# Layers 1 and 2 of a four-layer graph network: values and scores by seven block products, and six graphs in flight

## The chip, the cores and the metric

The kernel runs on one NeuronCore of a Trainium2 chip. The metric is the device time of one execution in microseconds (us). Before the change it is 2376.73 us, the median of 3 runs (2376.35 to 2377.58).

## What is computed

The input is 32 graphs of 512 nodes with 256 features (`x`, float32) and a 512x512 adjacency of zeros and ones with about 3% ones (`adj`, int32). Four layers follow each other, each of the form `x = x + layer(relu(layernorm(x)), adj)`; the layers differ. Layer 0 is softmax attention with two convolutions, layer 3 has a full bilinear score. Layers 1 and 2 are the ones that the change touches:

```
# layer 1                                   # layer 2
Wh = h @ W.T                                Hh = h @ W
src, dst = Wh @ a1, Wh @ a2                 s, d = Hh @ a_src, Hh @ a_dst
e = leaky(src[:,None] + dst[None,:])        e = exp(-leaky(s[:,None] + d[None,:]))
e = where(adj > 0, e, -9e15)                e = where(adj != 0, e, 0)
x = x + softmax(e) @ Wh                     x = x + elu((e @ Hh) / rowsum(e))
```

For each node a layer needs a value row (256 numbers) and two scores. Both are one product: the weight matrix is widened by two columns, W times a1 and W times a2, so that `h @ [W | Wa]` gives 258 columns.

## The kernel before, in words

A node tile is 128 nodes on 128 partitions, so a graph has NT = 4 tiles; the features are HC = 2 halves of 128. Everything is float32 on the TensorE. One Python function, `graph(b, ...)` (L467), lists the work of graph b as operations with an engine, a cost, what they follow, and the buffers that they use. A planner (`Plan`, L53) then lays all 32 graphs out: `order` (L131) keeps a clock per engine, gives each operation a due time worked back from its graph's number, and takes on each engine the most urgent operation whose inputs and buffers are there. The costs of L32 to L50 and the `SLACK` factors of L67 are what it plans with. The result is a fixed order of instructions for each engine; on the chip each engine goes through its own list in that order, and waits on semaphores.

The buffers are counted. `slot` (`FLIGHT` = 5, L243) says how many graphs may be between their first step and their store; `ahead` is one more and is for inputs loaded early. 35 `page`s of 4 KB for each partition hold nearly everything: x, normalized rows, transposed features, masks, exponentials. `v` are 4 value buffers, `bank` the 8 PSUM banks.

**One layer of a graph.** `normed` (L527) makes statistics on VectorE, a power on GpSimd, the normalized rows on ScalarE, and transposes them through a split into 16-bit planes (VectorE L551), a DMA transpose (SP queue, L554) and a join on ScalarE (L566) into `hT`. For layers 1 and 2, `scored_values` (L659) then makes four products, one for each node tile and all independent of each other: two accumulating matmuls of 258 columns (L669) into one PSUM bank, from which ScalarE copies 256 columns of values to `v` (L676) and VectorE the two score columns to a score buffer (L673). `leaky_exp_t` (L683) makes a row of scores over all nodes: in most graphs VectorE transposes 32x32 blocks (L697), and a DMA writes the row to DRAM (L701) and another spreads it to all partitions (L706); in the first two and last two graphs TensorE transposes instead (L693). ScalarE adds the other score and applies the leaky slope (L710) and the exponential (L713). VectorE masks: layer 1 takes the minimum with `mask1` (L934), a tile that VectorE makes once for each graph out of the transposed codes `codeT` (L931); layer 2 compares the codes directly (L961). `attend` (L726) multiplies: for each of 4 node tiles four times one matmul of 257 columns (L736; 256 values and a column of ones that yields the row sum).

**Products by blocks.** The other products (layer 0's and all of layer 3's) use `seven` (L592): a product of 2x2 blocks with seven block products in place of eight, in two PSUM banks p and q. Its order is fixed: product 1 into p, out; product 6 onto p, out; product 7 onto p, out; product 4 onto p, out, each waiting until the one before has been copied out of p by ScalarE; products 2, 5 and 3 go into q, and VectorE adds q onto the blocks. `block_sums` (L624) makes the four sums of input blocks that this needs, on VectorE (L639), three of them one after another. `seven_of` (L388) makes the seven weight blocks once at the start. `by_nodes` (L779) is the block product with nodes as rows: two matmuls of 128 or 129 columns (L783).

A float32 `nc.tensor.matmul` call leaves two MATMUL records and two LDWEIGHTS records in the trace, so a count in the profile is twice the number of calls.

Of the kernel before, what the change touches and what calls it, by code (L numbers as in the profile page):

```python
# [11 lines left out]
F32 = mybir.dt.float32  # L12
# [7 lines left out]
P = 128  # L20
# [4 lines left out]
HUGE = 2.0**100  # L25
# [27 lines left out]
class Plan:  # L53
# [13 lines left out]
    SLACK = {"V": (1.05, 0.0), "A": (1.05, 0.0), "G": (1.5, 0.0), "D": (1.0, 800.0)}  # L67
# [138 lines left out]
def kernel(  # L206
# [36 lines left out]
    FLIGHT = 5  # L243
    PAGES, VALUES = 35, 4
# [107 lines left out]

    def transposed(w_sb, dst, after, *keys):
        done = []
        for c in range(HC):
            key = f"bank{next(banks)}"

            def turn(c, key):
                for r in range(HC):
                    nc.tensor.transpose(W[key][:, r * P : (r + 1) * P], w_sb()[:, r, c * P : (c + 1) * P], ident)  # L360

            def out_of(c, key):
                nc.vector.tensor_copy(dst()[:, c, :], W[key][:, : HC * P])
# [45 lines left out]
    l1_aug, l2_aug = (tile_of(n, H + 2) for n in ("l1_aug", "l2_aug"))  # L409
# [5 lines left out]
    for n, dst, w, key in (("w0", w0_s, w0, "raw9"), ("att", att_s, att_w, "raw10")):  # L415
# [9 lines left out]
    l3_wide = raw("raw8", H + 2)  # L425
    a = [load(l1_sb, rows_of(l1_w), "raw0")]
    ready["l1"] = transposed(l1_sb, lambda: l1_aug[:, :, :H], a, "raw0")
    a += [load_column(l1_ac, l1_a.rearrange("n o -> (n o)"))]
    ready["l1"] += product(lambda d: l1_aug[:, d, H : H + 2], l1_sb,
                           lambda c: l1_ac.rearrange("p (o c) -> p c o", o=2)[:, c, :], 2, a, "raw0")  # L430
    a = [load(l2_aug[:, :, :H], rows_of(l2_w))]
    a = ready["l2"] = a + transposed(lambda: l2_aug[:, :, :H], l2_wt, a, "raw1")
    a = a + [load_column(l2_ac, l2_a.rearrange("o n -> (o n)"))]
    ready["l2"] = a + product(lambda d: l2_aug[:, d, H : H + 2], l2_wt,
                              lambda c: l2_ac.rearrange("p (o c) -> p c o", o=2)[:, c, :], 2, a, "raw1")
# [23 lines left out]

    score_bufs = []  # L460
    for i in range(FLIGHT):
        s = const.tile([P, P + NT], F32, tag=f"scores{i}", name=f"scores{i}")
        nc.gpsimd.memset(s, 0.0)
        score_bufs.append(s)


    def graph(b, adj_before, x_before):  # L467
# [42 lines left out]
        def classes(g):  # L510
            nc.vector.tensor_scalar(T["code"][:, two(g), :], T["adj"][:, two(g), :], -1.0, 2.0, ALU.max, ALU.min)
# [9 lines left out]
        def mask0():  # L521
            nc.vector.tensor_scalar(T["mask0"], T["codeT"], 1.0, TINY, ALU.is_equal, ALU.max)
# [132 lines left out]
        def scores_of():  # L655

            return score_bufs[T.places["slot"]["number"]]
# [528 lines left out]
```

## Time and profile before

| | |
|---|---|
| median of 3 runs | 2376.73 us |
| the profiled execution, its own time | 2375.45 us |
| its span, first to last instruction | 2373.7 us |
| mean granted TensorE clock | 0.999 |
| busy: TensorE, VectorE, ScalarE, GpSimd | 2347.7, 2056.8, 1720.1, 251.6 us |
| share of the span | 99%, 87%, 72%, 11% |
| chain that ended last, by engine | PE 94%, DVE 3%, ACT 2% |
| moved by DMA | 178.72 MB, mean 75 GB/s |

Times in the profile are of one execution. The profile has, first, busy time for each engine, and the span in 40 slices with the busy tenths of each engine in each. PE is TensorE's matmuls, PEld its weight loads, DVE VectorE, ACT ScalarE, POOL GpSimd, and SP the engine that issues most DMAs. Then come groups of instructions: line, engine, operation, what is written and read, shape and count, the busy time, the mean length of one in ns, and the idle time ahead of them with what ended it. "Busy" counts time in which at least one instruction of an engine is under way, so two that overlap are not counted twice, and a mean length can be more than the step from one start to the next. The timeline merges equal neighbours into one line with a count. The table of stretches gives each engine's busy time and, in brackets, its number of instructions between two times. A wait names the engine that ended it.

### The profile page before, as it was taken

What the parts mean: (1) busy time and instruction counts of PE and PEld (TensorE: products, weight loads), DVE (VectorE), ACT (ScalarE), POOL (GpSimd) and SP (SyncE); (2) the same over time, 40 slices, a digit from 0 to 9 for tenths busy, and PEclk for the clock granted to TensorE, in tenths of its full rate; (3) what the DMA queues carried; (4) which work ended last, traced back from release to release, by engine and by line L of the source; (5) the groups of instructions that cost most, each with busy time, mean ns of one, the idle gap of its engine ahead of it and who ended that gap; (6) DMA issues with size and microseconds to landing.
All of it is one profiled execution on the core that took longest, in us unless ns stands there. A gap on an engine that the chain in (4) does not pass through costs nothing.

```text
span 2373.7 us, 36569 instructions
## 1 busy us (share of the span) xinstructions
PE 2347.7 (99%) x11590; PEld 1985.6 (84%) x11590; DVE 2056.8 (87%) x6330; ACT 1720.1 (72%) x3386; POOL 251.6 (11%) x319
## 2 busy tenths in 40 slices
PE   7999999999999999999999999999999999999998
PEld 5887888888888888888888888888888888888887
DVE  6787899888898888988888988889888889888799
ACT  4566777777777777777777777777777777766785
POOL 3000010111001010101110111001011100100110
PEclk9999999999999999999999999999999999999999
DMA  7421332333333233332323334233233333321221
GB/s 188 94 54 30 87 86 65 85 79 69 85 70 89 69 67 87 78 84 70 85 61 85 74 72 87 65 85 78 66 88 77 71 83 74 89 54 41 49 47 43
DMA packets 432017, 178.72 MB, mean 75 GB/s; under 512 B 386288, under 2 KB 403824, under 8 KB 431824
## 3 DMA queue, kind: packets, MB, share of 16 engines
q1 hardware_dynamic: 426464, 158.03, 29.8%
q0 software_dynamic: 5216, 18.23, 2.3%
q8 instruction: 92, 1.51, 0.3%
q14 instruction: 101, 0.83, 0.1%
q10 hardware_dynamic: 144, 0.13, 0.0%
HBM read 67.64 MB, written 16.89 MB: 36 GB/s over the span
## 4 chain that ended last, share of the span: by engine, by line
PE 94%; DVE 3%; ACT 2%; DMA 0%; issue 0%; SPq 0%; POOL 0%; DVEq 0%; ACTq 0%
PE bank_a L736 35%; PE bank_z L893 9%; PE bank_v L669 9%; PE bank_o L911 5%; PE bank_s3p L1025 5%; PE bank_q0p L848 4%; PE bank_f3p L757 4%; PE bank_v0p L783 4%; PE bank_f0p L757 4%; PE bank_w3p L783 4%; PE bank_q0q L848 3%; PE bank_s3q L1025 3%; PE bank_v3p L783 2%; PE bank_v3q L783 2%; ACT e L710 1%; ACT e L713 0%
## 5 line engine op out<-in xcount | busy, mean ns | idle before, releaser
L736 PE MATMUL bank_a<-v,e 128*128 128x257 f32 (+1 forms) x4096 | 979.8, 381 | 6.0 <-DVE e L823 3.0
L736 PEld LDWEIGHTS bank_a<-v,e 128*128 128x128 f32 x4096 | 758.3, 190 | 155.3 <-issue 55.3
L566 ACT COPY hT<-planesT 128x512 uint16<-128x512 uint16 x508 | 380.8, 766 | 52.0 <-DMA planesT<-planes 51.6
L539 POOL TENSOR_TENSOR rstd<-ve,mhalf 128x2 f32<-128x2 f32 x256 | 215.9, 871 | 1875.1 <-DVE ve L536 1584.4
L546 ACT ACTIVATE xn<-x,off,rstd 128x256 f32<-128x256 f32 x512 | 276.0, 596 | 39.2 <-DVE off L542 39.0
L669 PE MATMUL bank_v<-l_aug,hT 128*128 128x258 f32 x1024 | 252.8, 381 | 2.1 <-ACT e L710 1.1
L893 PE MATMUL bank_z<-e,y 128*128 128x512 f32 x512 | 240.6, 592 | 0.0
L551 DVE COPY planes<-xn 128x512 uint16<-128x512 uint16 x508 | 205.7, 418 | 23.0 <-DMA planesT<-planes 17.2
L669 PEld LDWEIGHTS bank_v<-l_aug,hT 128*128 128x128 f32 x1024 | 191.7, 190 | 30.5 <-ACT e L710 1.5
L532 DVE BATCH_NORM_STATS2 st<-x 128x6 f32<-128x256 f32 x512 | 209.0, 408 | 4.1 <-DMA x<-in_x_dram 4.0
L710 ACT ACTIVATE e<-row,scores 128x512 f32<-128x512 f32 x224 | 150.7, 713 | 16.3 <-DMA row<-row 16.0
L893 PEld LDWEIGHTS bank_z<-e,y 128*128 128x128 f32 x512 | 96.9, 190 | 68.0 <-issue 57.9
L713 ACT ACTIVATE e<-e 128x512 f32<-128x512 f32 x256 | 150.3, 624 | 0.0
L676 ACT COPY v<-bank_v 128x256 f32<-128x256 f32 x256 | 90.2, 376 | 71.5 <-PE bank_v L669 67.7
L911 PE MATMUL bank_o<-w_sb,zT 128*128 128x256 f32 x512 | 116.2, 379 | 0.0
L1032 DVE SCALAR_TENSOR_TENSOR e<-bank_s3p,v,mask 128x256 f32<-128x256 f32 x256 | 111.2, 476 | 2.7 <-PE bank_s3p L1025 1.9
L533 DVE BATCH_NORM_AGGREGATE mv<-st 128x2 f32<-128x6 f32 x512 | 93.1, 182 | 17.5
L911 PEld LDWEIGHTS bank_o<-w_sb,zT 128*128 128x128 f32 x512 | 97.0, 190 | 13.4
L1077 ACT ACTIVATE e<-e 128x512 f32<-128x512 f32 x128 | 78.1, 629 | 22.7 <-DVE e L1074 22.0
L915 DVE SCALAR_TENSOR_TENSOR z<-bank_o,rs,b_sb 128x256 f32<-128x256 f32 x128 | 56.0, 479 | 40.7 <-PE bank_o L911 40.1
L974 ACT ACTIVATE y<-bank_a,rs 128x256 f32<-128x256 f32 x128 | 54.7, 476 | 49.4 <-DVE rs L970 25.9
L1071 ACT ACTIVATE e<-e,zero 128x512 f32<-128x512 f32 x128 | 84.9, 711 | 6.6 <-DVE crest L1049 6.6
(189 smaller groups left out, 4414.9 us busy)
## 6 DMA issues: line engine op xcount, KB each, us to landing
adj<-in_adj_dram SPq DMA_DIRECT2D x128, 256.0 KB
x<-in_x_dram SPq DMA_DIRECT2D x31, 512.0 KB
out_dram<-y POOLq DMA_DIRECT2D x31, 512.0 KB, 3.5
row<-row SPq DMA_DIRECT2D x56, 256.0 KB
planesT<-planes SPq DMA_TRANSPOSE x508
codeT<-code SPq DMA_TRANSPOSE x128
crest<-crest SPq DMA_TRANSPOSE x64
row<-sT SPq DMA_DIRECT2D x56, 2.0 KB
```

Of the source, the lines that this page charges most:

```text
L532: nc.vector.bn_stats(T[f"st{l}"][:, t, :], T["x"][:, t, :])
L539: nc.gpsimd.tensor_tensor(T[f"rstd{l}"][:, two(g)], T[f"ve{l}"][:, two(g)], mhalf[:, two(g)], ALU.pow)
L546: nc.scalar.activation(T[f"xn{l}"][:, t, :], T["x"][:, t, :], AF.Relu, bias=T[f"off{l}"][:, t : t + 1], scale=T[f"rstd{l}"][:, t : t + 1])
L551: nc.vector.tensor_copy(T[f"planes{l}_{t}"], bits)
L566: nc.scalar.copy(bits[:, :, :, t * P : (t + 1) * P], T[f"planesT{l}_{t}"].rearrange("p (b c) n -> p b c n", b=2))
L669: nc.tensor.matmul(T[key][:, :cols], T[f"hT{l}"][:, c, t * P : (t + 1) * P], w_aug[:, c, :], start=(c == 0), stop=(c == HC - 1))
L736: nc.tensor.matmul(T[key][:, : LEAD + H + 1 - lead], e(l, c)[:, t * P : (t + 1) * P], T[f"v{l}"][:, c, lead:], start=(c == 0), stop=(c == ...
L757: nc.tensor.matmul(p[:, : N // 2], w[:, x - 1, :], right(x), start=fresh, stop=True, skip_group_check=True)
L783: nc.tensor.matmul(p[:, j * k : (j + 1) * k], right(x)[:, j * P : (j + 1) * P], w[:, x - 1, :], start=fresh and j == 0, stop=True, skip_gr ...
L893: nc.tensor.matmul(T[f"bank_z{k}"], T["y0"][:, c, k * P : (k + 1) * P], e(0, c), start=(c == 0), stop=(c == NT - 1))
L911: nc.tensor.matmul(T[key][:, j * H : (j + 1) * H], T["zT"][:, k, t * P : (t + 1) * P], w1_sb[:, k, :], start=(k == 0), stop=(k == HC - 1))
L1025: nc.tensor.matmul(p[:, j * N // 2 : (j + 1) * N // 2], left(x)[:, j * P : (j + 1) * P], right(x), start=fresh and j == 0, stop=True, skip ...
```

## The change

- `scored_values` uses `seven` for layers 1 and 2, as layer 3's values did before: seven block products of two 129-column matmuls each in place of four tile products of two 258-column matmuls. The input sums (`block_sums`, four for each layer) are new there; layer 3's own code for this is now a call of the same function. The weights are cut into seven blocks of 129 columns at the start (`seven_of`), for which the raw weights are laid out 258 wide first; layer 2's weight load becomes two DMAs.
- Values and scores stay in one buffer: a row of `v` is [score, 128 values, score, 128 values, ones]. The score copies and the score buffers go. The block transpose, the TensorE transposes and the bias of the leaky step read `v`, and follow all four blocks, where they followed four score copies. `attend` reads 258 columns in layers 1 and 2 in place of 257, and the row sum stands one column further.
- The codes become `adj` times 2^96 (they were `adj` clipped to -1..2), so that layer 1 can mask straight from `codeT` in one operation (`max` with a tiny number, then `min`): `mask1` goes.
- `FLIGHT` 5 to 6, value buffers 4 to 5, pages 35 to 34. The planner's `SLACK` for VectorE and ScalarE goes from 1.05 to 1.0.

```diff
-HUGE = 2.0**100
+HUGE = 2.0**96
...
-    SLACK = {"V": (1.05, 0.0), "A": (1.05, 0.0), "G": (1.5, 0.0), "D": (1.0, 800.0)}
+    SLACK = {"V": (1.0, 0.0), "A": (1.0, 0.0), "G": (1.5, 0.0), "D": (1.0, 800.0)}
...
-    FLIGHT = 5
-    PAGES, VALUES = 35, 4
+    FLIGHT = 6
+    PAGES, VALUES = 34, 5
...
-    l1_aug, l2_aug = (tile_of(n, H + 2) for n in ("l1_aug", "l2_aug"))
+    l1_aug, l2_aug = (tile_of(n, HALF + 1, 7) for n in ("l1_aug", "l2_aug"))
...
+    ready["l1"] = seven_of(l1_wide, l1_aug, HALF + 1, t, "raw11")
...
+    ready["l2"] = seven_of(l2_wide, l2_aug, HALF + 1, a, "raw12")
...
         def classes(g):
-            nc.vector.tensor_scalar(T["code"][:, two(g), :], T["adj"][:, two(g), :], -1.0, 2.0, ALU.max, ALU.min)
+            nc.vector.tensor_scalar(T["code"][:, two(g), :], T["adj"][:, two(g), :], HUGE, None, ALU.mult)
...
-            nc.vector.tensor_scalar(T["mask0"], T["codeT"], 1.0, TINY, ALU.is_equal, ALU.max)
+            nc.vector.tensor_scalar(T["mask0"], T["codeT"], HUGE, TINY, ALU.is_equal, ALU.max)
...
-        def scored_values(l, hs, w_aug, ready):
-            cols = w_aug.shape[2]
-            vs, ss = [], []
-            for t in range(NT):
...
-                a = op("PE", pe(n258=4), [hs[t]] + ready, partial(product, t, key), key, f"hT{l}")
-                ss.append(op("V", V_TINY, [a], partial(scores, t, key), key))
-                vs.append(op("A", A_HALF, [a], partial(values, t, key), key, f"v{l}"))
-            return vs, ss
+        def scored_values(l, after, right, w, ready):
+            def block(i, l_):
+                return T[f"v{l}"][:, two(l_), i * (HALF + 1) : (i + 1) * (HALF + 1)]
+
+            def write(i, l_, key, start, after):
+                return op("A", A_HALF, after, lambda: nc.scalar.copy(block(i, l_), two_tiles(key, start, HALF + 1)),
+                          key, f"v{l}")
+
+            def add(i, l_, key, start, after):
+                return op("V", V_SUM, after, lambda: nc.vector.tensor_tensor(
+                    block(i, l_), block(i, l_), two_tiles(key, start, HALF + 1), ALU.add), key, f"v{l}")
+
+            return seven(f"v{l}", pe(nt=4), lambda x: after(x) + ready, (f"hT{l}", f"hs{l}"), partial(by_nodes, w, right),
+                         write, add)
...
-                nc.vector.transpose(T[f"sT{l}"], scores_of()[:, :P])
+                nc.vector.transpose(T[f"sT{l}"].rearrange("p (t j) -> p t j", t=NT), T[v][:, :, 0:32])
...
-            lead = LEAD if l < 3 else 0
+            lead = (LEAD, 1, 1, 0)[l]
...
-        def mask1():
-            nc.vector.tensor_scalar(T["mask1"], T["codeT"], HUGE, TINY, ALU.mult, ALU.max)
-
         def masked1(c):
-            nc.vector.tensor_tensor(e(1, c), e(1, c), T["mask1"][:, c, :], ALU.min)
+            nc.vector.scalar_tensor_tensor(e(1, c), T["codeT"][:, c, :], TINY, e(1, c), ALU.max, ALU.min)
...
         hs = normed(1, xs)
-        m1 = op("V", V_HALF, [m0, hs[0]], mask1, "codeT", "mask1")
-        vs, ss = scored_values(1, hs, l1_aug, ready["l1"])
-        es = leaky_exp_t(1, ss, 1.0)
-        es = [op("V", V_MASK, [a, m1], partial(masked1, c), "mask1", f"e1_{c // 2}") for c, a in enumerate(es)]
+        right_after, right = block_sums("hs1", "hT1", lambda j, l: T["hT1"][:, j, half(l)], hs, left=False)
+        vb = scored_values(1, right_after, right, l1_aug, ready["l1"])
+        vs = [tuple(vb.values())] * NT
+        es = leaky_exp_t(1, vs, 1.0)
+        es = [op("V", V_MASK, [a], partial(masked1, c), "codeT", f"e1_{c // 2}") for c, a in enumerate(es)]
```

Layer 2 is changed in the same way. Instructions in the two built programs, before and after: TensorE 5823 and 6207 matmul calls and others, VectorE 6332 and 6504, ScalarE 3389 and 3389, SP 982 and 982, GpSimd 324 and 321.

## The prediction

> **What bounds the kernel now.** I read the slices of the span first, then the table of stretches, then the timeline of TensorE, then the groups and waits. The slices say where to look:
>
> ```profile
> PE   7999999999999999999999999999999999999998
> DVE  6787899888898888988888988889888889888799
> ACT  4566777777777777777777777777777777766785
> PEclk9999999999999999999999999999999999999999
> ```
>
> TensorE is at nine tenths from the second slice on, at full clock; VectorE is close behind at eight, ScalarE has room. The table of stretches (start and end, then busy us and count for PE, PEld, DVE, ACT, POOL) sharpens that, for two stretches in the middle and for the last 44 us:
>
> ```profile
> 1025.00:1170.00 145.00, 145.00 (x722) 123.42 (x722) 128.19 (x394) 107.72 (x213) 15.56 (x18) 1.00 0.33 77
> 1315.00:1460.00 145.00, 145.00 (x719) 123.26 (x718) 129.63 (x401) 108.06 (x213) 15.94 (x18) 1.00 0.36 78
> 2330.00:2374.00 44.00, 37.08 (x199) 32.30 (x198) 39.42 (x91) 21.75 (x37) 1.50 (x2) 0.96 0.18 51
> ```
>
> Between 300 and 2040 us PE is busy for all but 0.07 us. The idle PE lies at the ends: 15.1 us of the first 300, 11.1 us of the last 334. In the last 44 us VectorE is the busier one. Busy can mislead for matmuls, so I check starts (timeline of PE, start and length of a merged piece):
>
> ```profile
> 1034.43 0.60 PE L757 MATMUL bank_f0p<-hs,att_s 128*128 128x256 f32 x2
> 1034.87 1.03 PE L669 MATMUL bank_v<-l_aug,hT 128*128 128x258 f32 x4
> 1035.74 0.59 PE L757 MATMUL bank_f3p<-hT,m 128*128 128x256 f32 x2
> 1036.17 0.59 PE L757 MATMUL bank_f0p<-hs,att_s 128*128 128x256 f32 x2
> 1036.60 0.61 PE L783 MATMUL bank_v3p<-l_aug,hs 128*128 128x129 f32 x4
> 1037.05 0.61 PE L783 MATMUL bank_v3q<-l_aug,hT 128*128 128x129 f32 x4
> 1037.49 1.03 PE L1025 MATMUL bank_s3p<-hT,fa 128*128 128x256 f32 x4
> ```
>
> From start to start, two records of 256 columns take 0.43 us (0.216 each), four of 258 take 0.87 (0.218 each), four of 129 take 0.445 (0.111 each), whatever stands beside them. So time goes by columns. With these steps the records of one ordinary graph come to 72.6 us: 128 in `attend` 27.8, 32 of the values 7.0, 16 of 512 columns at 0.43 give 6.9, 16 of L911 3.5, 56 of scores 12.1, 28 of features 6.0, 84 of 128 or 129 columns 9.3. Two graphs in 145 us: that is the rhythm of the middle. TensorE is full, back to back, and its work sets the time. The waits of PE agree; after the one of 9.1 us at the very start the longest are
>
> ```profile
> PE bank_a L736 <- DVE e L823: 3.0, 1, 3.0
> PE bank_a L736 <- ACT y L884: 2.2, 1, 2.2
> PE bank_v L669 <- ACT e L710: 1.1, 1, 1.1
> ```
>
> (total us, times, longest), all of them in the first 300 or last 334 us, and none is for layer 3's values, which already go by seven products.
>
> [...] The trace agrees that the 99% needs a check (a 258-column record is 381 ns long but steps by 218), and the starts above give it. [...] two records of 129 cost 222 ns against 218 for one of 258, so halving costs about 4 ns. [...] The trace shows the turns of v3p at 1033.54, 1036.60, 1038.79 and 1040.97, with other graphs' work between, so the wait was covered.
>
> **The change part by part.** The rows for it (groups: busy, mean ns, then idle before):
>
> ```profile
> L676 ACT COPY v<-bank_v 128x256 f32<-128x256 f32 x256 | 90.2, 376 | 71.5 <-PE bank_v L669 67.7 <-PE bank_a L736 2.1 <-DVE scores L673 1.3
> L1012 ACT COPY v<-bank_v3p 128x258 f32<-128x258 f32 x128 | 48.0, 375 | 41.0 <-PE bank_v3p L783 40.2
> L639 DVE TENSOR_TENSOR hs<-hT,hs 128x256 f32<-128x256 f32 x126 | 51.8, 415 | 0.1
> L1015 DVE TENSOR_TENSOR v<-v,bank_v3q 128x258 f32<-128x258 f32 x96 | 39.8, 416 | 4.2 <-PE bank_v3q L783 2.2
> L673 DVE COPY scores<-bank_v 128x2 f32<-128x2 f32 x256 | 35.6, 151 | 15.8 <-ACT v L676 7.6 <-PE bank_v L669 6.6
> L931 DVE TENSOR_SCALAR mask<-codeT 128x2048 bf16<-128x2048 bf16 x32 | 21.7, 677 | 0.0
> ```
>
> *TensorE, on the path.* A layer's values are now 16 records of 0.218 = 3.49 us. After: 7 products of 4 records, 28 of 0.111 = 3.11 us. Saved 0.38 us, times 64 (two layers, 32 graphs) = 24 us. The timeline is rounded to 0.01 us; with 0.217 for the wide record (257 and 258 columns step alike in most pieces) and 0.1113 for the narrow one it is 22.8; I take 23.5. Against it, 32 records of a layer in `attend` grow by one column: 0.43 us for 512 against 0.216 for 256 is 0.83 ns a column, so 32 times 64 times 0.83 ns = 1.7 us. Net: minus 22 us (bounds 21 and 22.5). Set-up transposes only change their source.
>
> *ScalarE.* Four copies of 376 ns become four of 375: nothing, same count in the built programs. Their place changes: each now stands between two products on bank p. Behind the waiting product stands the whole fixed list of TensorE, other graphs' work included; the cover is that work, placed between by the planner. If it is missing, a turn costs the copy and the hand-over, at least 0.4 us. In the built order the turns are mostly parted by 1 to 2 us of other products; early in the run (graph 0 and 1) some are parted by one. I take 0 in the middle; the upper end is in rival B.
>
> *VectorE, beside it.* For each graph: 8 sums of 0.415 (+3.32), 6 additions of 0.416 (+2.50), less 8 score copies of 0.151 (-1.21) and `mask1` of 0.677: +3.9 us. Back to back, instructions step by some 0.08 us less than their length (two L639 in 0.75), and then it is +3.5. Layer 1's masking, 682 ns as L934, becomes the form of L961, 680 ns: nothing. The codes, 683 ns with two operations, keep shape and types with one: I take no change; not below 0 by more than a few ns, and at most double, +1.4 us a graph, which rival A holds. The block transpose (303 ns) reads a strided source: 0, at most another 0.3 us. VectorE goes from 64.0 us a graph (the 145-us stretches have 126 to 130 for two) to 67.5 to 67.9, and TensorE from 72.6 to 71.9: VectorE at 94%. It doesn't set the rhythm, but is near.
>
> *Waits and queues.* The row of scores now follows four blocks, where it followed four tile products. Both take long: v3's seven products spread from 1033.5 to 1046.6, layer 1 and 2's tile products from 1028.3 to 1044.0. A sum or two of 0.4 us ahead comes to that. With six graphs in flight there is one more graph to fill it. Row DMAs, input loads and transposes on SP keep their numbers (982); one more weight DMA on GpSimd (0.8 us of its time, as L1139) and four memsets less lie in the first 60 us, before layer 1 needs weights at 68.7. Set-up cuts on VectorE, two times six operations of about 0.28 us, 3.3 us, lie there too; uncovered they cost 3.3.
>
> *The ends.* The start keeps its chain (input, statistics, codes); a sixth graph may fill a little: 0 to -3. At the end TensorE has idle time and VectorE is the busier, on layer 3's work, which isn't touched. Three graphs' added VectorE work ahead of it is at most 11.7 us, but between 2040 and 2330 VectorE has some 40 us free. Estimate +4 us, one graph's added work, bounds -3 and +11.
>
> *Sum.* Profiled time 2375.45 (span 2373.7 and 1.75 around it) - 22 + 4 = 2357.5. The median of the runs lies 1.3 above the profiled run: 2358.8, say 2359.
>
> **The rivals.**
>
> *A, slower: VectorE becomes the bound.* Place: the middle; mechanism: its fixed list, at 67.7 us of busy time a graph, can't be run at 94%, and TensorE waits for masks, sums and evacuations. Price: at a sustained 92% the rhythm is 67.7/0.92 = 73.6 us, 1.0 more than now, for some 28 graphs in the middle +28 us: 2376.7 + 28 = 2405. It makes the kernel slower from the point where VectorE can't hold 67.7/72.6 = 93.3%. For it: the last 44 us, where VectorE leads, reach only 39.42/44 = 89.6%, and the margin in the plan is gone. Against it: VectorE's longest waits are for TensorE (65.8 us in 68 waits of L944 for `attend`), so it is ahead, and dense runs need less than the lengths say.
>
> *B, a smaller gain: the turns on bank p aren't all covered.* There are 5 hand-overs a layer, three on p through ScalarE and two on q through VectorE, so 320 in a run. If one in four lacks 0.12 us of cover, that is 80 times 0.12 = 10 us: 2369. If all lacked 0.1 it would be 32 us. Against it: v3, v0, q0 and s3 do this now with no wait of PE in the middle.
>
> *C, no difference:* pages are fewer and needed more (hs1 and hs2, against mask1), so the plan starts graphs later and most of the gain goes into bubbles of PE: 2374. For it: each layer holds two banks and a page more for the length of its seven products, some 13 us as v3's. Against it: PE has no bubble in the middle now, with five graphs, and `mask1`'s page comes free.
>
> **How the numbers follow.** Forecast 0.70 (2353 to 2365, from its end bounds), B 0.14 (2365 to 2372), C 0.05, A 0.11. About 0.2%, 4.8 us, is what can be told from no change: faster is below 2372: 0.84; the same 0.05; slower 0.11. The range leaves out A, C and the lower tail: 2352 to 2372.
>
> **What would show it.** Right: 28 records of 129 columns for a layer stepping by 0.111, PE busy 145.00 in the middle stretches, two graphs in 143.8 us, VectorE near 135 of 145. Wrong: PE idle in the middle ended by DVE sums, masks or `v` additions (A), or by ACT copies of `bank_v1p` (B); a tail longer than 11 us over now would break the end estimate.

## The result, and the profile after

| | before | after |
|---|---|---|
| median, 7 runs each on the same chip | 2376.73 us (2375.10 to 2377.88) | 2369.82 us (2367.68 to 2373.28) |
| profiled execution: own time, span | 2375.45, 2373.7 us | 2373.28, 2370.3 us |
| busy: TensorE, VectorE, ScalarE | 2347.7, 2056.8, 1720.1 us | 2335.9, 2137.2, 1695.6 us |

The ratio is 0.9974, with a 95% interval of 0.9963 to 0.9985: faster by 6.9 us, where 17.7 was forecast. The profiled execution of the kernel after is the slowest of its seven, 3.5 us over their median, and that of before lies 1.3 under its median. So the two traces differ by less than the medians do, and losses read from the trace of the kernel after may be some microseconds too large for an ordinary run.

The slices of the kernel after:

```profile
PE   7999999999999999999999999999999999999998
DVE  7878899998999998999999989998999999987998
ACT  4566787767777677876677766678777777766884
PEclk9999999999999999999999999999999999999999
```

VectorE has gone from eights to many nines, and TensorE looks as full as before. The slices are too coarse for a loss of 10 us. In the table of stretches (start and end, then busy us and count for PE, PEld, DVE, ACT, POOL; near the end of the line the granted clock) of the kernel after, those shown before are now

```profile
1025.00:1170.00 145.00, 144.53 (x771) 124.22 (x770) 132.03 (x402) 105.66 (x212) 15.72 (x18) 1.00 0.38 77
1315.00:1460.00 145.00, 144.53 (x773) 124.29 (x772) 130.74 (x395) 104.77 (x210) 12.83 (x16) 1.00 0.36 76
2330.00:2370.30 40.30, 33.92 (x188) 29.62 (x186) 34.57 (x80) 21.79 (x38) 1.50 (x2) 0.95 0.18 52
```

PE stands still for 0.47 of 145 us, in both. That is small and new. The last stretch has 6.4 us of PE idle; the forecast's had 6.9, of which 0.3 lie behind the end of the span. Three wider stretches, of the kernel before and then of the kernel after:

```profile
0.00:80.00 80.00, 67.54 (x283) 50.08 (x284) 59.83 (x203) 44.23 (x83) 20.73 (x44) 0.98 0.65 168
80.00:300.00 220.00, 217.37 (x1045) 180.17 (x1044) 173.49 (x545) 147.98 (x294) 17.63 (x23) 1.00 0.28 62
300.00:2040.00 1740.00, 1739.93 (x8624) 1479.61 (x8623) 1537.02 (x4726) 1293.53 (x2544) 183.54 (x216) 1.00 0.33 77
```

```profile
0.00:80.00 80.00, 65.77 (x279) 49.54 (x280) 62.66 (x220) 44.13 (x82) 21.28 (x43) 0.96 0.69 168
80.00:300.00 220.00, 216.11 (x1113) 180.89 (x1112) 179.80 (x550) 142.77 (x284) 17.68 (x21) 0.98 0.30 63
300.00:2040.00 1740.00, 1735.95 (x9247) 1490.18 (x9246) 1600.15 (x4864) 1275.13 (x2551) 183.54 (x218) 1.00 0.36 78
```

In the middle, VectorE's busy time went from 1537.0 to 1600.2 of 1740 us, from 88 to 92%. The products themselves do what the change says (timeline of PE in the kernel after):

```profile
1034.33 0.61 PE L781 MATMUL bank_w3p<-l_w1s,hT 128*128 128x128 f32 x4
1034.78 1.03 PE L730 MATMUL bank_a<-v,e 128*128 128x257 f32 x4
1035.64 0.61 PE L781 MATMUL bank_v2p<-l_aug,hs 128*128 128x129 f32 x4
1036.09 1.03 PE L730 MATMUL bank_a<-v,e 128*128 128x257 f32 x4
```

Four records of 128 or 129 columns step by 0.45 us. The longest waits of PE in the kernel after, over the whole run (total us, times, longest):

```profile
PE bank_n L563 <- ACT xn L550: 9.0, 1, 9.0
PE bank_a L730 <- ACT hT L570: 3.4, 1, 3.4
PE bank_f0p L755 <- ACT fa L763: 2.6, 2, 1.7
PE bank_f3p L755 <- ACT fa L765: 2.5, 6, 0.6
PE bank_v0p L781 <- ACT e L704: 1.9, 1, 1.9
```

The first is the start, as before. The other four are new among the longest, all end with ScalarE, and none is for the new products: for `bank_v1p` PE waits 0.2 us in all, for `bank_v2p` none. Two are for ScalarE's copies out of bank p in the features of layers 0 and 3 (`fa`), products that the change did not touch. Between 300 and 2040 us these two are nearly all that shows:

```profile
PE bank_f3p L755 <- ACT fa L765: 2.3, 5, 0.6
PE bank_f0p L755 <- ACT fa L763: 0.8, 1, 0.8
```

**A balance of steps.** Idle hides part of such losses, because a matmul record is drawn longer than its step (381 ns against 218), and a gap shorter than the difference does not show. So I took the time from each PE record's start to the next one's and subtracted the usual step of its width (0.429 us for 512 columns, 0.216 to 0.218 for 256 to 258, 0.111 for 128 and 129). The first column of the table is the sum of the usual steps; the rest is what the steps had too much, by where it lies; the last is the time from the last start to the end. Each line adds up to its span.

| us | work | before the first | 0–80 | 80–300 | 300–2040 | 2040 on | after the last | span |
|---|---|---|---|---|---|---|---|---|
| before | 2336.8 | 9.1 | 9.3 | 3.4 | 1.1 | 8.0 | 6.0 | 2373.7 |
| after | 2314.5 | 9.0 | 11.3 | 8.0 | 10.0 | 10.8 | 6.7 | 2370.3 |

The work fell by 22.3. Given back: 2.0 in the first 80 us, 4.6 from there to 300, 8.9 in the middle, 3.5 at the end. In the middle, 13 steps were over 0.15 us too long (6.2 us together, against one step and 0.2 us before), 22 were 0.05 to 0.15 too long (2.2 us), and the rest, 1.6 us, is spread over 9210 records. Sorted by the record that they stand ahead of, some 6.3 us of the 8.4 are ahead of `bank_f3p` and `bank_f0p` (4.3 and 2.0), the features of layers 3 and 0; 1.2 are ahead of `bank_w3p`, also of layer 3, and none of these steps is ahead of a bank of the new products. One of these turns, from the timeline of the kernel after:

```profile
1133.30 0.72 ACT L704 ACTIVATE e<-row,v 128x512 f32<-128x512 f32 x1 [1.12 <-DMA row<-row]
1133.93 0.46 ACT L765 ACTIVATE fa<-bank_f3p,l_u 128x256 f32<-128x256 f32 x1
1134.44 0.70 PE L755 MATMUL bank_f3p<-hs,m 128*128 128x256 f32 x2 [0.47 <-ACT fa L765]
```

The product ended at 1132.2 us. But ScalarE's fixed order has a row of scores ahead of the copy, and ScalarE stands 1.12 us for the DMA that brings this row. Four of the long turns have such a row just ahead of them and one has `planesT`; together they lost 3.5 us. Ahead of most of the others, ScalarE or VectorE was busy with what its order had first.

**One stall followed to its root.** ScalarE's longest standstill for a DMA between 80 and 300 us in the kernel after, from its timeline (start, length, in brackets the idle time ahead and what ended it):

```profile
151.58 0.68 ACT L854 ACTIVATE e<-e 128x512 f32<-128x512 f32 x1
155.97 0.77 ACT L570 COPY hT<-planesT 128x512 uint16<-128x512 uint16 x1 [3.72 <-DMA planesT<-planes]
```

What it waits for is a DMA transpose. The SP queue, which issues it, was doing this:

```profile
146.31 5.12 SPq L518 DMA_TRANSPOSE codeT<-code  x4
151.52 0.52 SPq L497 DMA_DIRECT2D adj<-in_adj_dram  x1
152.14 2.50 SPq L558 DMA_TRANSPOSE planesT<-planes  x2
```

The planes that this transpose reads, of graph 2's third node tile, were ready at about 143.5 us. But after two other transposes the fixed order of SP has graph 5's four code transposes and graph 6's input load first: from 146.31 to 152.14 us, 5.8 us. ScalarE, in its own fixed order, waits with score rows and copies of other graphs behind it, and PE then waits for those:

```profile
160.11 0.71 PE L781 MATMUL bank_v0p<-w_s,hT 128*128 128x128 f32 x4 [1.90 <-ACT e L704]
162.54 2.08 PE L755 MATMUL bank_f0p<-hs,att_s 128*128 128x256 f32 x4 [1.72 <-ACT fa L763]
```

The clock falls too. From 161.7 us, within the second of these pauses, to 168.5 us the granted clock is a half (same kernel, table of stretches):

```profile
150.00:161.00 11.00, 8.92 (x51) 7.33 (x49) 8.88 (x26) 7.28 (x14) 0.00 (x0) 1.00 0.61 145
161.70:168.50 6.80, 5.96 (x16) 4.96 (x17) 4.05 (x17) 2.23 (x8) 0.69 (x1) 0.51 0.00 0
168.50:180.00 11.50, 11.50 (x70) 10.46 (x70) 7.05 (x23) 6.39 (x14) 0.00 (x0) 1.00 0.23 24
```

The timeline of PE shows it in the steps:

```profile
165.26 1.92 PE L730 MATMUL bank_a<-v,e 128*128 128x257 f32 x4
166.98 1.07 PE L781 MATMUL bank_v1p<-l_aug,hT 128*128 128x129 f32 x4
```

Four records of 257 columns take 1.72 us, 0.43 each in place of 0.217. By the balance the 16 records of this stretch lost 3.0 us and the two pauses 4.0, together most of the 8.0. What starts the half speed here and sets its 6.8 us isn't shown.

The time at half speed isn't the same in every execution. The mean granted clock is 0.996 in the profiled one and 0.998 in three of the other six, which is, by an estimate from these means and the span of 2370 us, at least some 5 us less at half speed. So a part of what this trace lost may go with the execution and not with the order.

### The profile page after: what moved, and what is told of

Read it like the earlier page. It is cut to its first block, busy times and chain, and to the rows that moved or that the text cites. A ratio compares the mean times of both kernels' runs of the same rounds, so it can differ in the third digit from the quotient of the medians.

```text
span 2370.3 us, 38073 instructions
## 1 busy us (share of the span) xinstructions
PE 2335.9 (99%) x12358; PEld 1993.8 (84%) x12358; DVE 2137.2 (90%) x6502; ACT 1695.6 (72%) x3386; POOL 250.1 (11%) x316
## 4 chain that ended last, share of the span: by engine, by line
PE 84%; ACT 6%; DVE 5%; DMA 3%; issue 1%; SPq 0%; POOL 0%; DVEq 0%; ACTq 0%
PE bank_a L730 32%; PE bank_z L891 8%; PE bank_s3p L1013 4%; PE bank_q0p L846 4%; PE bank_v0p L781 4%; PE bank_f3p L755 4%; PE bank_o L909 4%; PE bank_w3p L781 4%; PE bank_f0p L755 3%; PE bank_q0q L846 3%; PE bank_s3q L1013 3%; PE bank_v3p L781 2%; PE bank_v1p L781 2%; PE bank_v2p L781 2%; DMA planesT<-planes 2%; PE bank_v3q L781 2%
## 5 line engine op out<-in xcount | busy, mean ns | idle before, releaser
L730 PE MATMUL bank_a<-v,e 128*128 128x258 f32 (+2 forms) x4096 | 1027.8, 382 | 6.5 <-ACT hT L570 3.4
L730 PEld LDWEIGHTS bank_a<-v,e 128*128 128x128 f32 x4096 | 744.6, 191 | 109.1 <-issue 11.3
L704 ACT ACTIVATE e<-row,v 128x512 f32<-128x512 f32 x224 | 156.0, 721 | 10.4 <-DMA row<-row 10.2
L707 ACT ACTIVATE e<-e 128x512 f32<-128x512 f32 x256 | 157.2, 633 | 0.0
L891 PEld LDWEIGHTS bank_z<-e,y 128*128 128x128 f32 x512 | 91.6, 191 | 64.2 <-issue 57.4
L667 ACT COPY v<-bank_v1p 128x258 f32<-128x258 f32 x128 | 48.0, 375 | 95.4 <-PE bank_v1p L781 95.0
L1062 DVE TENSOR_TENSOR e<-e,crest 128x512 f32<-128x512 f32 x128 | 84.3, 684 | 33.7 <-ACT crest L1056 33.7
L854 ACT ACTIVATE e<-e 128x512 f32<-128x512 f32 x93 | 58.8, 632 | 73.8 <-DVE e L863 73.7
L643 DVE TENSOR_TENSOR hs<-hT 128x256 f32<-128x256 f32 x254 | 99.9, 414 | 10.6 <-ACT hT L570 10.3
L643 DVE TENSOR_TENSOR hs<-hT,hs 128x256 f32<-128x256 f32 x254 | 105.5, 415 | 0.2
L1059 ACT ACTIVATE e<-e,zero 128x512 f32<-128x512 f32 x128 | 88.9, 724 | 17.4 <-DVE crest L1037 16.7
L929 DVE SCALAR_TENSOR_TENSOR e<-codeT,e 128x512 f32<-128x512 bf16 x128 | 86.8, 683 | 15.7 <-ACT e L707 15.6
```

Source lines behind the costliest of these rows:

```text
L643: nc.vector.tensor_tensor(d(x), first, second, how)
L730: nc.tensor.matmul(T[key][:, : LEAD + H + 1 - lead], e(l, c)[:, t * P : (t + 1) * P], T[f"v{l}"][:, c, lead:], start=(c == 0), stop=(c == ...
L891: nc.tensor.matmul(T[f"bank_z{k}"], T["y0"][:, c, k * P : (k + 1) * P], e(0, c), start=(c == 0), stop=(c == NT - 1))
```

## The experiments

The theories. V: VectorE, at 92% in the middle, is late, and TensorE waits for it (rival A at a small size). P: the plan has no margin left, with `SLACK` at 1.0 for VectorE and ScalarE. D, from the second group on: DMAs land later than planned, ScalarE stands for `planesT`, and others behind it. The letter R has two senses. In the expectations of the first two groups, and for the moves by hand, it says that the ends of the run, the first 300 us above all, decide. From `PASS` 210 on it says: no step is too dear; the planner's fixed order falls well or badly, and this one fell badly. Below, R is meant in this second sense.

The losses below are from the same balance of steps, each from the profiled execution of that kernel. Nearly every edit also makes the planner draw another order, so one run says little about its own cause unless the effect is large; the table at the end shows the scatter. Ratios are to the kernel before as it was run beside each group: 2376.23 us for the first four runs, 2375.83 for the next four, 2376.58 for the four after, 2375.59 for the last four.

### The plan and the load

**The margin back.** `SLACK` as before the change:

```diff
-    SLACK = {"V": (1.0, 0.0), "A": (1.0, 0.0), "G": (1.5, 0.0), "D": (1.0, 800.0)}
+    SLACK = {"V": (1.05, 0.0), "A": (1.05, 0.0), "G": (1.5, 0.0), "D": (1.0, 800.0)}
```

> The changed kernel with the planner's SLACK for VectorE and ScalarE back at 1.05; nothing else. Now TensorE stands idle 4 us in the middle (300 to 2040 us), 18 in the first 300 and 13 at the end. Theory P (the plan has no margin, so that ScalarE's waits for transposes reach TensorE): the middle idle falls under 1 us and the time to some 2363. Theory V (VectorE's load itself, 92% busy, is what delays): the middle stays at 4 or more, the time within 2 us of 2370. Theory R (the ramp: what the order does in the first 300 us and in the last ones decides): the middle may change by a few us, but most of the difference is in the ends, in either direction, up to 6 us.

Measured: 2375.7 us, ratio 0.9998 (0.9990 to 1.0006). The loss of the middle doubled, from 10.0 to 20.1 us, and that from 80 to 300 us fell to 0.5. None of the three theories had this time. P isn't borne out for the middle: with 5% more planned time it was worse.

**Five graphs in flight.**

```diff
-    FLIGHT = 6
+    FLIGHT = 5
```

> The changed kernel with five graphs in flight in place of six; value buffers and pages stay. Theory R (the sixth graph's loads crowd the first transposes): the start's idle falls from 18 to some 15 us and the half-speed clock after it goes, 2362 to 2366. Theory of cover (five graphs don't fill the longer chains): middle idle rises from 4 to over 10 us, 2378 or more. Theory P and V: little changes, 2368 to 2372.

Measured: 2393.74 us, ratio 1.0079 (1.0066 to 1.0091). The middle loses 28.8 us, and the longest of its waits is PE on bank p of the features behind a VectorE sum (4.2 us in 8 waits). That is more than in any of the orders with six graphs, which speaks for the sixth graph: with five, this kernel is 17 us slower than the kernel before.

**Less work for VectorE.** The six additions onto `v` of layers 1 and 2 touch two elements of each partition; the rest of these sums is left out:

```diff
             def add(i, l_, key, start, after):
+                if l < 3:
+                    return op("V", (66.0, 151.0), after, lambda: nc.vector.tensor_tensor(
+                        block(i, l_)[:, :, :1], block(i, l_)[:, :, :1], two_tiles(key, start, HALF + 1)[:, :, :1], ALU.add), key, f"v{l}")
                 return op("V", V_SUM, after, lambda: nc.vector.tensor_tensor(
```

> The changed kernel in which the six additions of bank q onto the values of layers 1 and 2 touch 2 elements a partition and not 258: the rest of these sums is left out, the instruction and its waits stay. VectorE has some 1.6 us less in each graph, about 50 us in all; the planner knows it. TensorE's work is the same. Theory V: the middle idle goes to under 1 us and the time falls to 2361 to 2364. Theory P and R: the middle stays at 3 to 5 us, as the waits for transposes and loads stay; the time 2366 to 2372, by chance of the order.

Measured: 2365.73 us, ratio 0.9960 (0.9946 to 0.9973). Its middle in the table of stretches:

```profile
300.00:2040.00 1740.00, 1736.39 (x9249) 1489.76 (x9248) 1570.16 (x4868) 1270.16 (x2551) 185.37 (x218) 1.00 0.35 78
```

VectorE has 30 us less in the middle (1570 against 1600), and PE's busy time there hardly moves (1736.39 against 1735.95; loss 9.3 against 10.0). The 4 us came from 80 to 300 us (8.0 to 3.6). That speaks against V, and V's forecast of under 1 us of idle time in the middle is missed.

**The plan alone, on the kernel before.**

```diff
-    SLACK = {"V": (1.05, 0.0), "A": (1.05, 0.0), "G": (1.5, 0.0), "D": (1.0, 800.0)}
+    SLACK = {"V": (1.0, 0.0), "A": (1.0, 0.0), "G": (1.5, 0.0), "D": (1.0, 800.0)}
...
-    FLIGHT = 5
+    FLIGHT = 6
```

> The kernel before with the planner's two settings of the change alone: SLACK 1.0 and six graphs in flight (pages 35, value buffers 4 and all work as before). Theory P: the margin is what kept the middle free of idle time, so some 3 to 6 us of it appear: 2379 to 2383. Theory V: VectorE is at 88%, so the middle stays at 0: 2376 to 2378. Theory R: the start gains 2 to 5 us of idle time and slow clock by six graphs' loads: 2379 to 2382, with the middle at 0.

Measured: 2391.54 us, ratio 1.0066 (1.0053 to 1.0078). In the middle PE is busy for all of the 1740 us, so neither the missing slack nor six graphs starve it there; but it loses 13.8 us between 80 and 300, and 13.8 from 2040 on (before: 3.4 and 8.0). In this order the plan alone costs 15 us, more than any of the three theories allowed.

### The landings, VectorE with more work, the start, the codes

**Twice the margin for DMAs.** In the planner each DMA lands 1600 ns later than its own length, in place of 800:

```diff
-    SLACK = {"V": (1.0, 0.0), "A": (1.0, 0.0), "G": (1.5, 0.0), "D": (1.0, 800.0)}
+    SLACK = {"V": (1.0, 0.0), "A": (1.0, 0.0), "G": (1.5, 0.0), "D": (1.0, 1600.0)}
```

> The changed kernel whose planner counts every transpose and load on the SP queue as landing 0.8 us later (the D entry of SLACK from 800 to 1600 ns); all work as in the changed kernel. Theory D (in the middle ScalarE stands in its fixed order before a transpose or a row that lands later than planned, and the feature copies behind it reach TensorE late): ScalarE's waits for transposes in the middle fall from 82 us to under 40, TensorE's idle time there from 4 us to under 1, and the run to 2362 to 2366 if the ends stay. Theory V (VectorE's load): middle stays at 3 to 5, 2368 to 2374. Theory R (the ends): the middle may fall, but the ends move by as much in either direction.

Measured: 2364.32 us, ratio 0.9951 (0.9939 to 0.9964). ScalarE's wait for `planesT` over the whole run, in the kernel after and then here:

```profile
ACT hT L570 <- DMA planesT<-planes: 109.2, 87, 6.1
```

```profile
ACT hT L570 <- DMA planesT<-planes: 25.8, 28, 3.8
```

The wait that D blames is down by three quarters, and the middle loses as much as before (11.1 us). So D falls as the cause in sum; that the time lies in D's range is luck. As far as the trace tells, none of the long turns in the middle stands behind a late DMA here, where five did in the kernel after; but others, mostly of `bank_f0p` behind busy work of ScalarE or VectorE, have come in their place. From 80 to 300 us the loss went from 8.0 to 0.6, but so it did in most of the other orders (the table below), so that is no proof of D either.

**More work for VectorE.** A mask that nobody needs, once for each graph, ahead of layer 1's masking:

```diff
-        es = [op("V", V_MASK, [a], partial(masked1, c), "codeT", f"e1_{c // 2}") for c, a in enumerate(es)]
+        m1 = op("V", V_HALF, [m0, hs[0]], lambda: nc.vector.tensor_scalar(
+            T["mask1"], T["codeT"], 1.0, TINY, ALU.mult, ALU.max), "codeT", "mask1")
+        es = [op("V", V_MASK, [a, m1], partial(masked1, c), "codeT", f"e1_{c // 2}") for c, a in enumerate(es)]
```

> The changed kernel with the mask1 step put back, unused: one VectorE instruction of 0.6 to 0.7 us more in each graph, about 20 us in all, and its page; the planner knows it. VectorE in the middle goes from 92 to 93%. Theory V: TensorE's idle time in the middle rises from 4 to over 10 us, 2378 or more. Theory D: it stays at 3 to 6, 2368 to 2374.

Measured: 2358.60 us, ratio 0.9929 (0.9916 to 0.9941). The middle of this kernel:

```profile
300.00:2040.00 1740.00, 1738.65 (x9271) 1494.59 (x9270) 1620.08 (x4911) 1278.42 (x2565) 189.19 (x218) 1.00 0.35 78
```

With 20 us more of VectorE work in the middle (1620 against 1600, 93%) TensorE is busier, its loss there is halved (5.0), and the kernel is 11 us faster than the kernel after. V is refuted as the bound: TensorE lost less with more load. D's range, 2368 to 2374, is missed as well. What the useless mask does besides is to shift the plan, which is where R in its second sense comes from.

**The start.** Graph 1's loads of `adj` follow the transposes of graph 0's codes, not only the codes:

```diff
-        return code, got_x[-1]
+        return (tuple(coded) if b == 0 else code), got_x[-1]
```

> The changed kernel with graph 1's adjacency loads made to follow the transposes of graph 0's codes, as they stand in the kernel before: the load that splits the four transposes moves behind them. Theory R: the first product of graph 0's attention starts near 31.8 us and not at 33.8, the idle time of the first 80 us falls by 2 to 3 us, slow clock there halves; 2365 to 2368 if the rest stays. Rival (the ramp is bound by VectorE and by the loads in sum): the gain at 33.8 is lost again before 300 us; 2368 to 2372.

Measured: 2364.19 us, ratio 0.9954 (0.9942 to 0.9967). The first 80 us gave only 0.7 (11.3 to 10.6). The gain was again in 80 to 300 us (8.0 to 0.1), which this edit wasn't meant for, and the middle stayed at 11.1.

**The codes alone, on the kernel before.** `adj` times 2^96 and no `mask1`:

```diff
-            nc.vector.tensor_scalar(T["code"][:, two(g), :], T["adj"][:, two(g), :], -1.0, 2.0, ALU.max, ALU.min)
+            nc.vector.tensor_scalar(T["code"][:, two(g), :], T["adj"][:, two(g), :], HUGE, None, ALU.mult)
...
-            nc.vector.tensor_tensor(e(1, c), e(1, c), T["mask1"][:, c, :], ALU.min)
+            nc.vector.scalar_tensor_tensor(e(1, c), T["codeT"][:, c, :], TINY, e(1, c), ALU.max, ALU.min)
```

> The kernel before with one part of the change alone: codes are the adjacency times 2 to the 96th, layer 1 masks straight from them, mask1 goes. VectorE has some 0.7 us less a graph, TensorE the same work. All theories have the middle free of idle time: 2374 to 2378, no difference but what the order does at the ends.

Measured: 2376.50 us, ratio 1.0003 (0.9995 to 1.0011). VectorE has 24 us less in the middle (1513 against 1537), and the time doesn't move: in the kernel before, this part of VectorE's work lies beside TensorE's.

### Other orders of the same work

**Moving a few operations by hand.** The order of the kernel after, with graph 2's two plane transposes put ahead of graph 5's code transposes on SP, and graph 5's mask put eight places back on VectorE:

```diff
+    for t, codes in ((2, 0), (3, 2)):
+        o = order.pop(at("turn", 2, t, l=1))
+        order.insert(at("turn_code", 5, codes), o)
+    o = order.pop(at("mask0", 5))
+    order.insert(at("masked2", 0, 3) + 1, o)
```

> The changed kernel's own order with three moves and nothing else: two transposes of graph 2's layer 1 on the SP queue move ahead of four of graph 5's code transposes (one of them ahead of two) and of graph 6's load, and graph 5's mask on VectorE moves eight instructions back. It takes away the 3.7 us for which ScalarE stands before such a transpose at 152 us. Theory R: the idle time of TensorE between 80 and 300 us falls from 3.9 to under 1 and the half-speed clock after it goes; in sum 5 to 7 us: 2363 to 2365. Rival (the ramp's stall is made by all queues together and shifts to another place): 2367 to 2371.

Measured: 2367.79 us, ratio 0.9965 (0.9953 to 0.9978). From 80 to 300 us the loss is 4.4 in place of 8.0: in this trace the half clock at 161.7 us is gone (the granted clock from 80 to 300 us is 1.00, where it was 0.98), which was 3.0, and the pause of 1.90 us is down to 0.4, but PE still stands for 1.7 us ahead of `bank_f0p`. So the moves took away a part of the stall. Which of the three did it isn't separated, and the half clock differs between executions too. The gain on the kernel after, 2.0 us, is too small to be told from none: the intervals of the two ratios overlap. The middle stays (10.4).

**One constant, 5% off.** `PASS` (L61) is the time in ns that the planner puts between the end of an operation and the start of one that waits for it; due times are worked out with it too, and no instruction changes:

```diff
-    PASS = 200.0
+    PASS = 210.0
```

> The changed kernel with one constant of the planner 5% off (PASS 210 in place of 200 ns): the same work in another order. If what an order happens to bring in the ramp and in the middle decides over some us, as theory R has it, this gives another time than 2370, anywhere from 2356 to 2372, with the work on TensorE equal to 1 us. If the changed kernel has a cost of its own that takes 11 us (theories V, D and P), it gives 2368 to 2372.

Measured: 2358.65 us, ratio 0.9925 (0.9913 to 0.9938). Two stretches of this kernel:

```profile
80.00:300.00 220.00, 220.00 (x1158) 185.96 (x1158) 186.14 (x574) 148.34 (x294) 19.76 (x23) 1.00 0.29 64
300.00:2040.00 1740.00, 1738.87 (x9275) 1494.98 (x9274) 1605.93 (x4885) 1279.33 (x2561) 205.07 (x218) 1.00 0.34 78
```

PE has no idle between 80 and 300 us, and loses 3.8 in the middle (three steps over 0.15 us too long, 1.6 us together, against 13 and 6.2). VectorE is as busy as in the kernel after. ScalarE even waits longer for `planesT` in the middle, 114.5 us against 81.6, which speaks against D once more. So 11 us of the kernel's time go with the order alone: the instructions are the same.

**The same constant on the kernel before.** Same edit.

> The kernel before with the same constant 5% off. If orders scatter there as well, the time is anywhere from 2370 to 2385; if VectorE's 88% leave enough cover for any order in the middle, the middle has under 1 us of idle time and the difference lies in the first 300 and last 330 us.

Measured: 2373.89 us, ratio 0.9989 (0.9980 to 0.9997). The same edit gains some 2.7 us here, so the 18 us of the run above aren't the constant's.

**Mask and start together.** The edits of the run with the useless mask and of the run on the start.

> The changed kernel with both edits that gained: the unused mask1 step and graph 1's loads behind graph 0's code transposes. If each removes its own stall, the gains add where they differ: 2354 to 2358. If both only draw another order, 2358 to 2368.

Measured: 2360.54 us, ratio 0.9936 (0.9923 to 0.9948). Edits that gave 11.2 and 5.6 us on the kernel after give 9.3 together. Most of both gains was the same, from 80 to 300 us, so they couldn't simply add; but there each alone had left 0.3 and 0.1 us of loss, and both together leave 2.7. Two local repairs would not do that, while two draws of an order may.

### Margin, flights, and two more orders

The stalls of the middle might still come from hand-overs that the plan takes for punctual (M), or from too few graphs in flight (K), and the orders so far might be lucky. Four more:

**300 ns on each hand-over** of VectorE and ScalarE, without more planned occupancy:

```diff
-    SLACK = {"V": (1.0, 0.0), "A": (1.0, 0.0), "G": (1.5, 0.0), "D": (1.0, 800.0)}
+    SLACK = {"V": (1.0, 300.0), "A": (1.0, 300.0), "G": (1.5, 0.0), "D": (1.0, 800.0)}
```

> After with 300 ns planned on top of each VectorE and ScalarE operation's hand-over (not on its occupancy). Theory M (the middle's small stalls come from hand-overs through ScalarE and VectorE that the plan takes for punctual, and a little latency margin would remove them): the loss between 300 and 2040 us falls from 10 to under 3, the time to 2356 to 2361. Theory R (an order is good or bad by what falls together in it; a margin is only one more order): anywhere in 2358 to 2372, and the middle's loss between 3 and 12. Theory P in its first form stays refuted by the run with 1.05.

Measured: 2373.16 us, ratio 0.9991 (0.9983 to 0.9999). The middle loses 14.4, the end 17.4 in place of 10.8. M, which had under 3 for the middle, isn't borne out; the range given for R (3 to 12, up to 2372 us) is missed too, by a little. In this order some 5.3 us of the middle stand ahead of `bank_v2p`, a bank of the new products.

**`PASS` 190 and 220.**

> After with the planner's PASS constant at 190 in place of 200: the same instructions in another order. Theory R: somewhere in 2358 to 2372, with the loss of the middle between 3 and 12 and that of 80 to 300 us between 0 and 8; the kernel after, at 2370, would be at the slow edge of such orders. Rival (the smaller PASS is itself worse and the larger better, in order of size): above 2372.

> After with PASS at 220: the same instructions in another order. Theory R: somewhere in 2358 to 2372, not better than the 210 for a reason of size. Rival (larger PASS is better in order of size, since it gives the flights more room): below 2358, the middle's loss under 3.8.

Measured: 2359.87 us, ratio 0.9936 (0.9923 to 0.9948), and 2360.50 us, ratio 0.9939 (0.9927 to 0.9952). With 190 the middle loses 8.9 and 80 to 300 us 0.1; with 220 it is 3.9 and 4.0. All three neighbours of the constant that the kernel has are 9 to 11 us faster than it, and there is no trend in their size: R holds, both rivals fall. As `PASS` is itself a margin on every hand-over, 10 ns less and 10 or 20 ns more gaining the same speaks against M again.

**Seven graphs in flight.**

```diff
-    FLIGHT = 6
+    FLIGHT = 7
```

> After with seven graphs in flight in place of six. Theory K (the middle still lacks other graphs' work to fill the turns of the seven products; five flights lost 29 us there, six lose 10): the middle falls under 4, the time to 2356 to 2362. Rival (pages, not flights, are short, so a seventh graph can't start): within 3 us of another order of the kernel after, 2360 to 2372, or slower if the start grows crowded.

Measured: 2381.60 us, ratio 1.0025 (1.0014 to 1.0037). The first 80 us lose 17.0 (11.3 in the kernel after) and the middle 17.8. K isn't borne out: in this order a seventh graph costs time at the start and the middle loses more, not less.

The same seven-product values in the orders tried (none of these edits takes work away), by time:

| edit on the kernel after | median us | lost 80–300 | lost 300–2040 |
|---|---|---|---|
| mask of no use | 2358.60 | 0.3 | 5.0 |
| `PASS` 210 | 2358.65 | 0.1 | 3.8 |
| `PASS` 190 | 2359.87 | 0.1 | 8.9 |
| `PASS` 220 | 2360.50 | 4.0 | 3.9 |
| mask and start | 2360.54 | 2.7 | 3.6 |
| start | 2364.19 | 0.1 | 11.1 |
| landings 1600 | 2364.32 | 0.6 | 11.1 |
| three moves by hand | 2367.79 | 4.4 | 10.4 |
| none | 2369.82 | 8.0 | 10.0 |
| 300 ns on hand-overs | 2373.16 | 0.5 | 14.4 |
| `SLACK` 1.05 | 2375.70 | 0.5 | 20.1 |

## Why the prediction was right or wrong

**TensorE's work: right.** Forecast minus 22 us (21 to 22.5); the sum of the usual steps fell by 22.3. The step of 0.111 us holds; how the 22.3 splits between narrower products and wider `attend` lies within the rounding of the steps.

**VectorE: not the bound, as forecast; its added busy time came out about a third lower.** 80.4 us more busy over 32 graphs is 2.5 a graph, where 3.5 to 3.9 was forecast, and the stretches of 145 us have 131 to 132 where 135 was. The single terms have their prices: sums 414 and 415 ns, additions 412 to 416, layer 1's mask 683 in place of 682, codes 684 in place of 683, block transpose 302 in place of 301. The lengths of all VectorE instructions, added up, rose by 120.7 us, which is 3.8 a graph, as forecast. Busy time counts an overlap once, so the 40 us between the two sums are instructions that overlap more. Rival A's bound does not appear: the run with 20 us more of VectorE work in the middle is among the two fastest. Nor does rival C's, 2374 us for want of pages: orders with the same 34 pages reach 2358.65.

**The step that failed: "I take 0 in the middle".** The middle lost 8.9 us more than before, in some 35 steps. The place wasn't the one that rival B named: the turns of `bank_v1p` and `bank_v2p` cost PE 0.2 us, covered as the forecast said. It was the same kind of turn in other products: some 6.3 of the 8.4 us in the long steps are ahead of bank p of the features of layers 0 and 3. The waits that show there (2.3 and 0.8 us) all end with ScalarE's copies. The copies came late because ScalarE's fixed order had something else first: in five of the turns, 3.5 us, a step that stood for a late DMA. Rival B's time, 2369, was met to within a microsecond, but by this neighbouring mechanism, so the agreement is luck. The forecast looked at the hand-overs that the change adds, and not at what its new order does to those that were there. Even the best orders in the table lose 3.6 to 3.9 us in the middle, where the kernel before lost 1.1.

**The second one: "a sixth graph may fill a little: 0 to -3" at the start.** The first 80 us lost 2.0 more and the next 220 lost 4.6 more. The latter is the stall at 152 us, with the clock's half speed behind it: in this order the sixth and seventh graph's loads and transposes stand in SP's queue ahead of what graph 2 needs. The forecast noted that SP's instructions "keep their numbers" and took that for no cost; what counts is whose turn it is. And it had no term for the half clock, which added 3.0 us to pauses of 3.6. It goes with this order, and in part with this execution: seven of the ten other orders in the table lose 0.1 to 0.6 us between 80 and 300 us. What the first 80 us lost stays untraced; the run on the start got 0.7 of it back.

**The ends: right.** Forecast +4; from 2040 us on and after the last start it was 2.8 and 0.7.

**What the runs settle.** The same instructions give 2358.65, 2359.87 and 2360.50 us at the three neighbouring constants, and 2359 was forecast; the kernel as handed over is some 10 us over those, by its order. But the agreement with 2359 is in part luck. With `PASS` at 210 the middle still lost 2.7 us more than before, and the stretch from 80 to 300 us lost 3.3 less: two misses that cancel. Nor are these three typical of all: the median of the eleven orders in the table is 2364.19 us. A forecast of this change would have had to give the order a range of its own.

**What stays open.** What makes an order good in the middle. Load, planning slack, hand-over margin, late landings and a seventh graph were each tried and none accounts for it. But slack, margin and the seventh graph were tried in one order each, and for the middle orders scatter from 3.6 to 20.1 us. In the kernel before, four orders lost some 1 to 3.5 us there. So the change may make the middle more sensitive to its order, whether by VectorE's 92% or by the turns that it adds; no run separates these. Whether the plan (six graphs, slack 1.0) and the products need each other isn't shown either: the plan alone cost 15 us and five graphs 17, each in one order. The cause of the stall at 152 us was shown in part only (4.4 of 8.0 us stay after the moves by hand).

The best version is the kernel after with `PASS` at 210 (2358.65 us); `PASS` 190 and 220 can't be told from it, nor can the one with the useless mask (2358.60), which does needless work.

## What to carry to other kernels

Where a planner fixes the order of all engines, a change has two prices: its instructions, which a sum of steps gave here to within a microsecond, and the order that comes out, which here scattered over 17 us for the same instructions. Try a few values of a planner constant before judging such a change, and put that scatter into the range of a forecast. Follow a stall back from TensorE through ScalarE to the queue that issues the DMA, and ask what stands ahead of it there.

## What the runs showed of the hardware that was not expected

- At two pauses of TensorE of 1.90 and 1.72 us, 0.7 us of work between them, the granted clock fell within the second one to 0.51 for 6.8 us, in which records of 257 columns stepped by 0.43 us and not 0.217.
- Idle in the profile showed 4.05 of the 10.0 us that the steps of the middle lost in the kernel after; the rest is in gaps shorter than the length that a record is drawn beyond its step (381 ns against 218).
- Four DMA transposes of codes took 5.12 us of SP's queue at 146.31 us in the kernel after, some 1.28 us each, against 0.52 us for the load of `adj` behind them. This load and the next transposes started 5.2 and 5.8 us after the first of the four.
